# A new table of shifts in the order of a conv-attention block on one core

## The chip, the core and the metric

The kernel runs on one core of one Trainium2 chip. A core has five engines with a queue of instructions each: TensorE (PE in the profile, with its weight loads as PEld), VectorE (DVE), ScalarE (ACT), GpSimd (POOL) and SyncE (SP, which here only issues DMAs). They work at the same time and wait for each other through semaphores; each takes its own instructions strictly in the order in which they were written. The metric is the device time in microseconds of one execution, as the median of several runs.

## The reference

The input `x` is 16 images of 128 channels and 96 x 96 pixels in fp32. Per image:

```python
xn1 = layernorm(x)                       # over the channels of each pixel
q, k, v = xn1 @ wq.T, xn1 @ wk.T, xn1 @ wv.T     # 8 heads of 16 channels
q, k = l2norm(q), l2norm(k)              # over the 9216 pixels
attn = softmax(q @ k.T * 16 ** -0.5)     # 16 x 16 per head
x = x + (attn @ v) @ wp.T
xn2 = layernorm(x)
h1 = w_in @ xn2                          # 128 -> 512 channels
h2 = conv3x3(h1, w_dw)                   # one filter per channel, zero padding
x = x + w_out @ gelu(h2)                 # 512 -> 128 channels
```

The attention is over channels: its matrix is 16 x 16 per head and has to be summed over all pixels of an image before it can be applied to any.

## The kernel before

An image is cut into 8 bands of 12 rows (1152 pixels), a band into 3 units of 4 rows (384 pixels). Three streams of work run interleaved over the whole kernel:

- **First norm and attention of the next image** (`norm(i, False)`, line 789, and `attention`, line 997). A band is loaded by SP (`load_a`), transposed by PE (`forth_a`), copied by ACT (`copied_a`), its statistics taken by DVE (`stats_a`), the inverse deviation made by POOL (`variance_a`, `power_a`) and applied (`scaled_a`); PE adds it to a Gram matrix (`gram`) and transposes it back (`back_a`), and ACT places it in a ring of rows in SBUF (`place_a`).
- **Second norm of the image at hand** (`norm(i, True)`): PE applies the attention as one 128 x 128 matrix (`mix`), ACT moves the result to SBUF (`mixed`), a DMA that POOL issues adds `x` to it (`add_x`), and then come `forth_b`, `stats_b`, `variance_b`, `power_b`, `back_b` and `place_b`, the last on DVE.
- **The feed-forward part**, in *jobs*: one job is one band and one chunk of 128 of the 512 hidden channels (`conv_job`, line 1133). PE makes the hidden rows (`hidden`, line 1152), ACT copies them out of PSUM (`kept`, line 1157, and `halo`, line 1148, for rows shared with the next band). The nine taps of the 3 x 3 filter are shared among engines: two or three, sometimes four, are made by ACT as products (`products`, line 1168) into buffers `pr`; POOL adds the first of them to the middle tap (`merge`, lines 1171 and 1174); DVE makes the others one after the other in PSUM (`tap`, lines 1180 and 1184), the first of them on top of the merged tile, and the last into a buffer `h3`; two DMAs issued by POOL add the rest, one product to another (`add_last`, line 1193) and their sum to `h3` (`add_first`, line 1196). ACT then applies GELU (`gelu`, line 1201). In some bands the fourth chunk is made by nine matmuls on PE instead (`by_matmuls`, line 1249: `conv` and `conv_gelu`, with the bias of the first and last column applied by ACT from a tile `edge`). Finally PE multiplies all four chunks by `w_out` (`out`, line 1300), DVE adds the result to `x` (`add`, line 1307), and SP stores the band (`store`).

There are 467 jobs. Buffers are few: 4 PSUM banks `h` for PE's results, 8 `pr`, 8 `h3`, 4 `zT`, 5 + 2 bands of `x`.

**The order.** The program is not written in the order in which it runs. Every piece is handed to a planner (`Plan`, line 223) with its engine, an estimated duration, what it reads and writes, and a *place*. `Plan.order` (line 269) plays the execution through with those estimates: when an engine is free, it takes from the pieces that are ready the one with the lowest place; buffers are handed out in the order of the places too. The order so found is then emitted, and on the chip each engine follows it as a fixed list, whatever the real durations are.

The place of a piece is made in `place_at`, line 546: the number of the job beside which it belongs, plus a constant for its kind (`AT`), plus a *shift* for its kind in this stretch of 15 jobs (`SHIFTS`), and a `RANK` that counts for the engine but not for the buffers.

```python
def place_at(kind, place, i=1):
    of = kind if i else kind + "_0"
    return Place(place + (AT[of] + SHIFTS.get(max(0, int(place // STRETCH)), {}).get(of, 0)), RANK.get(kind, 0))
```

A stretch spans 15 places, while many of the constants and shifts are hundreds or thousands: so within a stretch the kinds of one engine are in most cases strictly ranked, and a shift takes effect where it moves a kind past another kind of the same engine. For `out` and `hidden` on PE, for example, `AT` has 421.1 and 416.95. For `add_first` and `merge` on POOL it has -1420.85 and -380.8.

Of the kernel before, what the change touches and what calls it, by code (L numbers as in the profile page):

```python
# [51 lines left out]
    load_w=-385.3, weights=-616.15, zeros=-141.7, load_a=-42.4, forth_a=-588.2, stats_a=1671.35, variance_a=269.75,  # L52
# [14 lines left out]
    0: dict(load_w=-0.4, weights=5.2, zeros=-2.2, load_a=1.4, forth_a=-37.4, stats_a=-4.5, variance_a=-15.2,  # L67
        power_a=-1.9, merge=29.7, scaled_a=690.3, gram=-4.7, place_a=179.4, attention=-230.7, mix=-831.2,
        residual=407.9, mixed=-700.9, stats_b=8.5, variance_b=533.1, power_b=17.1, back_b=0.1, place_b=508.2,
        kept=1387.1, products=-11.5, add_last=-9.9, tap=-0.8, add_first=-4.2, gelu=16.5, conv=-3.5, conv_gelu=1.4,  # L70
        out=0.1, add=-1520.8, store=-31, mix_0=46.9, residual_0=637.6, gram_0=-6.5, forth_a_0=1.3, forth_b_0=1.7,
        stats_b_0=1195.7, scaled_a_0=1.5, copied_a=-135, back_a_0=1.7, back_b_0=-17.1, place_a_0=-6.5, late=-10.3,
        load_a_0=1.9, load_dw=15.2, units=-13.6, variance_a_0=49.8, power_a_0=-208.3, variance_b_0=5.2,
        power_b_0=545.9),
    1: dict(load_a=0.9, forth_a=-9.5, stats_a=-0.1, variance_a=121.4, power_a=-0.2, merge=7.6, scaled_a=1062.4,
        gram=1.4, back_a=-389.8, place_a=-1619.2, attention=-0.8, mix=-12.3, mixed=433.4, add_x=767.6, forth_b=9.1,
        stats_b=-189.7, variance_b=-0.3, power_b=5.7, back_b=-0.2, place_b=-2, halo=-3.8, hidden=0.4, kept=2503.9,
        add_last=13.5, tap=0.1, add_first=-18.8, gelu=2.7, conv=6.5, conv_gelu=1.1, add=-969.7, store=315.5),
    2: dict(load_a=0.2, forth_a=1, stats_a=21, variance_a=148.9, power_a=-29.3, merge=3.4, scaled_a=224.7,
        gram=369.1, back_a=0.3, place_a=21.5, mix=0.5, add_x=761.8, stats_b=-602.5, variance_b=-0.6, power_b=221.3,  # L80
        back_b=-2.3, place_b=864.3, halo=60.3, kept=2.2, products=-0.4, tap=0.1, add_first=-63.4, gelu=48.9,
        conv=-1.5, conv_gelu=-0.2, out=-0.2, add=5.4, store=-860.5, copied_a=-16.2, copied_b=451.4),
# [4 lines left out]
    4: dict(load_a=0.4, forth_a=-0.8, stats_a=51.7, variance_a=-21.1, power_a=-8.5, merge=0.5, scaled_a=17.6,  # L87
        gram=2.7, place_a=24.1, mix=0.1, add_x=38.9, forth_b=-7, stats_b=608, variance_b=-3.1, power_b=-2,
        place_b=1309.5, halo=-1008.9, hidden=0.7, kept=-17.1, add_last=15.7, tap=-0.6, add_first=-2.4, gelu=-118.4,
        conv=-5.9, conv_gelu=-0.5, out=0.6, add=14.9, store=-14.5, copied_a=1563.7),  # L90
    5: dict(load_a=-0.3, forth_a=-1.1, stats_a=-4.6, variance_a=-285.1, power_a=20.3, merge=-1017.1,
        scaled_a=-11.2, gram=-3.8, back_a=4.5, place_a=13.1, attention=-1.5, mixed=-1.7, add_x=314.7, stats_b=-3.5,
        variance_b=2352.2, power_b=0.1, place_b=-11.9, halo=-12.3, kept=5.1, products=-0.1, add_last=61.6,
        tap=-1.5, add_first=-47.3, gelu=14.1, conv=0.9, conv_gelu=-1.2, out=-1, add=-1511.4, copied_a=-616.3,
        copied_b=-1294.4),
    6: dict(load_a=0.4, forth_a=-2.4, stats_a=-5.7, variance_a=-1678.1, power_a=-1.9, merge=0.8, scaled_a=1445.1,
        place_a=952, mix=-3, mixed=-0.4, add_x=28.1, forth_b=0.7, stats_b=-0.6, variance_b=819.8, power_b=-4,
        place_b=872.4, kept=2426.6, products=0.1, add_last=38.2, tap=-0.1, add_first=11, gelu=41.2, conv=-0.4,
        conv_gelu=0.2, out=13.2, add=565, store=-118.5, copied_a=-10.5),
    7: dict(load_a=1.9, stats_a=15.2, variance_a=-1.3, power_a=31.3, merge=-6.8, scaled_a=22.7, gram=-2644.1,  # L100
        back_a=-3.3, place_a=-207.8, attention=2.2, mix=-0.9, stats_b=4, variance_b=-5.6, power_b=277.8,
        place_b=1322.6, halo=4.2, kept=1343, products=1.2, add_last=18.7, tap=-0.3, add_first=-69.9, gelu=-2.4,
        conv=0.3, conv_gelu=-0.5, out=-0.6, add=-2068, store=1612, copied_a=412.3, copied_b=483.1),
    8: dict(load_a=7.2, forth_a=0.5, stats_a=-7.7, variance_a=11.4, power_a=-406.1, merge=-42.2, scaled_a=-0.4,
        gram=19.8, back_a=0.2, place_a=-12.5, mix=0.5, mixed=-562.6, add_x=779.6, forth_b=15.6, power_b=16.9,
        back_b=-1235.4, halo=-16.2, hidden=-0.6, kept=477.2, products=-0.2, add_last=8.3, tap=0.3, add_first=13.3,
        conv=3342, conv_gelu=0.1, add=-2.7, store=-3.9, copied_a=-3.4),
    9: dict(forth_a=0.4, stats_a=20.3, variance_a=4367.7, power_a=42.6, merge=-0.1, scaled_a=1020.8, gram=-4.3,
        back_a=-1129, place_a=1, mix=1.8, mixed=4.9, add_x=-38.6, forth_b=-0.3, variance_b=-9.2, power_b=64,
        back_b=0.1, place_b=-452.4, halo=6.1, kept=518.8, add_last=797.1, tap=0.1, add_first=58.8, gelu=0.8,  # L110
        conv=-3.1, add=-1766.3, store=7, copied_a=1422.9),
    10: dict(load_a=6.8, forth_a=0.9, variance_a=-29.3, power_a=1.7, merge=-7.6, scaled_a=1431.4, gram=10.5,
        place_a=0.2, mixed=113.1, add_x=581.8, forth_b=-1.8, stats_b=-0.6, variance_b=1573.4, power_b=1638.8,
        place_b=8.5, halo=13.6, hidden=-0.1, kept=12.3, add_last=482.1, tap=0.1, add_first=0.3, gelu=-0.1,
        conv_gelu=1.2, out=-0.2, add=7.3, store=-988, copied_b=53.2),
    11: dict(load_a=-2.7, forth_a=-4.3, stats_a=1830.9, variance_a=-291.5, power_a=37.2, merge=-23.5,
        scaled_a=-0.9, gram=-4.9, back_a=1.5, place_a=184.8, attention=-2.9, add_x=-2.7, stats_b=-201.5,
        variance_b=1.5, back_b=-0.3, place_b=1.9, halo=-4528.6, hidden=-1.1, kept=-260, products=-0.7,
        add_last=25.2, tap=0.5, add_first=-0.7, gelu=34.8, conv=-22.2, conv_gelu=0.7, add=-957.7, store=-1469.1,
        copied_a=-742.1),  # L120
# [1264 lines left out]
```

## Time and profile before

| | |
|---|---|
| median of three runs | 3978.27 us (3977.37 to 3985.19) |
| the profiled execution | 3984.49 us |
| its span, first to last instruction | 3982.8 us |
| mean granted clock of TensorE | 0.998 |
| instructions | 50,559 |
| moved by DMA | 777.37 MB, mean 195 GB/s |

The span is the time from the first to the last instruction of one profiled execution; the time of a run has a little around it. A row of a group names the line of the kernel, the engine, the operation, the tile written and the tiles read, the count, the busy time and the mean of one in ns, and then how long the engine stood idle just before such instructions and for whom. A row of the view by stretches gives the window, its length, and the busy time and instruction count of each engine, then the granted clock, the busy share of the 16 DMA engines and their GB/s. A row of the waits says which engine waited at which line for what, the total in us, how often, and the longest.

### The profile page before, as it was taken

What the parts mean: (1) busy time and instruction counts of PE and PEld (TensorE: products, weight loads), DVE (VectorE), ACT (ScalarE), POOL (GpSimd) and SP (SyncE); (2) the same over time, 40 slices, a digit from 0 to 9 for tenths busy, and PEclk for the clock granted to TensorE, in tenths of its full rate; (3) what the DMA queues carried; (4) which work ended last, traced back from release to release, by engine and by line L of the source; (5) the groups of instructions that cost most, each with busy time, mean ns of one, the idle gap of its engine ahead of it and who ended that gap; (6) DMA issues with size and microseconds to landing.
All of it is one profiled execution on the core that took longest, in us unless ns stands there. A gap on an engine that the chain in (4) does not pass through costs nothing.

```text
span 3982.8 us, 50559 instructions
## 1 busy us (share of the span) xinstructions
PE 3851.3 (97%) x16467; PEld 2484.8 (62%) x16467; DVE 3828.5 (96%) x4392; ACT 3604.9 (91%) x5478; POOL 3378.8 (85%) x3107
## 2 busy tenths in 40 slices
PE   8999999999999999999999999999999999999899
PEld 7566666666666666666666665666666666665555
DVE  7999999999999999999999999999999999999888
ACT  3999989989999999999999999998999999999887
POOL 5998889889898988988888898888988989888674
PEclk9999999999999999999999999999999999999999
DMA  3999999999999999999999999999999998999887
GB/s 99 185 202 211 190 204 194 207 191 196 212 191 213 205 193 206 199 214 196 190 204 201 209 195 193 208 197 202 199 194 202 201 211 183 217 197 182 178 168 165
DMA packets 191688, 777.37 MB, mean 195 GB/s; under 512 B 22208, under 2 KB 23616, under 8 KB 191424
## 3 DMA queue, kind: packets, MB, share of 16 engines
q0 software_dynamic: 151920, 622.33, 82.2%
q1 hardware_dynamic: 38784, 151.75, 10.3%
q8 instruction: 129, 2.11, 0.2%
q14 instruction: 135, 1.11, 0.1%
q10 hardware_dynamic: 720, 0.07, 0.0%
HBM read 148.85 MB, written 75.50 MB: 56 GB/s over the span
## 4 chain that ended last, share of the span: by engine, by line
PE 38%; DVE 14%; ACT 13%; DMA 8%; POOL 8%; issue 6%; POOLq 0%; DVEq 0%; ACTq 0%
PE h L1300 11%; PE h L1152 9%; PE h L1264 9%; DVE acc L1184 7%; ACT pr L1168 6%; DMA h<-pr 6%; DVE acc L1180 3%; PE h L808 3%; DVE h L1180 2%; PE h L954 2%; POOL merged L1171 2%; PE g L906 2%; ACT h L1157 2%; DMA pr<-pr 2%; PE h L858 2%
## 5 line engine op out<-in xcount | busy, mean ns | idle before, releaser
L1168 ACT ACTIVATE pr<-h,ratio 128x1152 f32<-128x1152 f32 x1494 | 1841.0, 1276 | 31.8 <-DMA h<-pr 9.9
L1184 DVE SCALAR_TENSOR_TENSOR acc<-h,ratio,acc 128x1152 f32<-128x1152 f32 (+1 forms) x1308 | 1810.3, 1384 | 7.7
L1171 POOL TENSOR_TENSOR merged<-pr,h 128x1152 f32<-128x1152 f32 x466 | 1236.7, 2654 | 112.4 <-DVE acc L1180 51.4
L1152 PE MATMUL h<-xn,winT 128*128 128x384 f32 (+2 forms) x2802 | 1083.0, 494 | 22.2 <-ACT h L1157 12.7
L1300 PE MATMUL h<-h,woutT 128*128 128x384 f32 x3072 | 1074.8, 488 | 9.0 <-ACT h L1157 4.9
L1264 PE MATMUL h<-xn,comp 128*128 128x380 f32 (+2 forms) x2430 | 895.1, 483 | 7.2 <-DVE st_b L866 2.6
L1300 PEld LDWEIGHTS h<-h,woutT 128*128 128x128 f32 x3072 | 569.0, 190 | 385.8 <-ACT h L1157 13.8
L1157 ACT COPY h<-h 128x384 f32<-128x384 f32 (+2 forms) x1401 | 654.2, 498 | 145.0 <-PE h L1152 141.9
L1180 DVE SCALAR_TENSOR_TENSOR acc<-h,ratio,merged 128x1152 f32<-128x1152 f32 x466 | 684.0, 1468 | 32.7 <-POOL merged L1174 16.6
L1152 PEld LDWEIGHTS h<-xn,winT 128*128 128x128 f32 x2802 | 497.7, 190 | 342.5 <-issue 35.8
L1201 ACT ACTIVATE h<-h,ksum 128x1152 f32<-128x1152 f32 (+1 forms) x586 | 617.7, 1086 | 70.8 <-DMA h<-pr 68.7
L1196 POOL DMA_DIRECT2D h<-pr x466 | 465.1, 999 | 252.5 <-DVE h L1180 56.8
L1180 DVE SCALAR_TENSOR_TENSOR h<-h,ratio,acc 128x1152 f32<-128x1152 f32 x467 | 655.1, 1403 | 3.4 <-PE h L1300 0.2
L1264 PEld LDWEIGHTS h<-xn,comp 128*128 128x128 f32 x2430 | 432.0, 189 | 242.7 <-issue 14.2
L1193 POOL DMA_DIRECT2D pr<-pr x466 | 484.5, 1057 | 86.3 <-ACT pr L1168 66.7
L875 POOL TENSOR_TENSOR ve_b<-ve_b,mhalf 128x4 f32<-128x4 f32 x288 | 369.0, 1282 | 8.6
L899 POOL TENSOR_TENSOR zT<-zT,ve_a 128x512 f32<-128x512 f32 x270 | 342.0, 1275 | 7.0
L875 POOL TENSOR_TENSOR ve_a<-ve_a,mhalf 128x4 f32<-128x4 f32 x288 | 333.3, 1165 | 13.5
L858 PE MATMUL h<-ident,x 128*128 128x128 f32 x2244 | 318.6, 276 | 26.9 <-ACT h L1157 8.2
L858 PEld LDWEIGHTS h<-ident,x 128*128 128x128 f32 x2244 | 261.7, 142 | 113.9 <-issue 33.7
L906 PEld LDWEIGHTS g<-zT 128*128 128x128 f32 x2160 | 272.9, 192 | 46.1 <-POOL zT L899 13.3
L808 PE MATMUL h<-xn,mwT 128*128 128x384 f32 x768 | 291.1, 491 | 10.1 <-ACT x L817 2.2
(187 smaller groups left out, 3947.3 us busy)
## 6 DMA issues: line engine op xcount, KB each, us to landing
pr<-pr POOLq DMA_DIRECT2D x466, 576.0 KB, 7.8
h<-pr POOLq DMA_DIRECT2D x466, 576.0 KB, 7.9
x<-in_x_dram SPq DMA_DIRECT2D x128, 576.0 KB, 7.3
out_dram<-x SPq DMA_DIRECT2D x127, 576.0 KB, 4.8
x<-in_x_dram POOLq DMA_DIRECT2D x123, 576.0 KB, 8.9
out_dram<-x SPq DMA_DIRECT2D x3, 192.0 KB, 1.9
h<-in_L_conv_w_in_dram SPq DMA_DIRECT2D x1, 256.0 KB, 3.3
h<-in_L_conv_w_out_dram SPq DMA_DIRECT2D x1, 256.0 KB, 3.5
```

The lines of the kernel that those rows point to most:

```text
L858: nc.tensor.transpose(d["pT", q][:, k, :], xt[:, j * P : (j + 1) * P], ident)
L875: nc.gpsimd.tensor_tensor(rstd, rstd, mhalf, ALU.pow)
L1152: nc.tensor.matmul(rows(ph), lhsT=winT[:, n, :], rhs=window(xn, r0 + r, e - r, 1), start=True, stop=True)
L1157: nc.scalar.copy(window(h1_, r, e - r, 1), rows(d.pop(("ph", r))))
L1168: nc.scalar.activation(to, shifted(t), AF.Copy, scale=ratio[:, n, t : t + 1])
L1171: nc.gpsimd.tensor_tensor(merged, d["pr", dma_taps[0]], shifted(UNIT), ALU.add)
L1180: nc.vector.scalar_tensor_tensor(to, shifted(t), ratio[:, n, t : t + 1], also, ALU.mult, ALU.add)
L1184: nc.vector.scalar_tensor_tensor(to, shifted(t)[:, lo:hi, cut], ratio[:, n, t : t + 1], to, ALU.mult, ALU.add)
L1193: nc.gpsimd.dma_start(out=d["pr", dma_taps[1]], in_=d["pr", t], accum_op=ALU.add)
L1201: nc.scalar.activation(h3, h3, AF.Gelu, bias=ksum[:, z, n : n + 1])
L1264: nc.tensor.matmul(d["pc"][:, lo:hi, cut], lhsT=comp[:, t, :], rhs=window(xn, r0 + dy, UR, dx)[:, lo:hi, cut], start=(t == order[0]), stop ...
L1300: nc.tensor.matmul(rows(d["po"]), lhsT=woutT[:, n, :], rhs=h3s[g, n][:, s * UR : (s + 1) * UR, :], start=(k == 0), stop=(k == NCH - 1),)
```

## The change

Only `SHIFTS` (line 66) is replaced, by a table of the same form: 32 stretches, about 30 kinds in each. All other constants, the functions and the computation are the same. Of 1021 entries that either table has, 1005 differ; 242 entries of the old and 361 of the new are larger than 100 either way. Two stretches of the old and the new table in full, the last lines of stretch 0, and the shift of `add_first` where it went up most:

```diff
     0: dict(
...
-        load_a_0=1.9, load_dw=15.2, units=-13.6, variance_a_0=49.8, power_a_0=-208.3, variance_b_0=5.2,
-        power_b_0=545.9),
+        copied_a=-1469.5, back_a_0=-4.7, back_b_0=8.2, place_a_0=184.5, place_b_0=-6.4, late=-53.4, load_dw=3811.7,
+        units=36, variance_a_0=3610.5, power_a_0=-1224.6, variance_b_0=-20.3, power_b_0=1317.8),
...
-    3: dict(load_a=4.1, stats_a=-23.7, variance_a=-225.4, power_a=762, merge=-499.1, scaled_a=275.8, gram=17.8,
-        place_a=-222.9, attention=2.7, mix=-2.4, mixed=507.5, add_x=722, forth_b=6.4, stats_b=-607.4,
-        variance_b=1.6, power_b=208, place_b=4, halo=-5114.5, kept=1.1, products=0.1, add_last=-33.4,
-        add_first=-2.7, gelu=-3397, conv=-9, conv_gelu=-0.6, add=568.1, store=-17.6, copied_a=1164.2),
+    3: dict(load_a=4.1, forth_a=1.7, stats_a=-4, variance_a=149, power_a=1353.6, merge=22.5, scaled_a=-15.5,
+        gram=-37.3, place_a=-606.9, attention=3, mix=-3.3, add_x=364.7, forth_b=2.6, stats_b=-15.6, variance_b=-1,
+        power_b=-35.1, back_b=-419.8, halo=-4560.9, hidden=-409.4, add_last=351.8, add_first=1417.6, gelu=-2921.3,
+        conv=-6.4, conv_gelu=0.3, add=-12.8, store=-0.3, copied_a=-12.1),
...
-    29: dict(mix=-1.5, mixed=-15.9, add_x=-4.2, forth_b=-32.8, stats_b=-24.1, variance_b=1162.7, power_b=2838.3,
-        back_b=17.8, place_b=-6.3, halo=43.2, hidden=224.5, kept=-25.7, products=-1.3, add_last=34.8, tap=-0.2,
-        add_first=0.2, gelu=-4563.5, conv=-9.6, conv_gelu=1.1, out=170.7, add=-3.3, copied_b=-13.3),
+    29: dict(merge=-1.4, mix=13.3, mixed=-1627, add_x=3.2, forth_b=-12.1, stats_b=-1151.7, variance_b=0.8,
+        power_b=-29.4, back_b=50.4, place_b=906.3, halo=-4600.5, hidden=-475.1, kept=1529.1, products=2,
+        add_last=1967.8, tap=1.3, add_first=4901, gelu=-4636.8, conv=2.3, conv_gelu=0.4, out=194.6, add=-1787.8,
+        store=-629.6, copied_b=51),
```

| stretch | `add_first` before | `add_first` after | `merge` before | `merge` after |
|---|---|---|---|---|
| 3 | -2.7 | 1417.6 | -499.1 | 22.5 |
| 7 | -69.9 | 338.8 | -6.8 | -1050.5 |
| 15 | 10.4 | 1826.8 | -369.3 | -4.9 |
| 16 | -3.3 | 1473.5 | 337.1 | 23.5 |
| 18 | -64.3 | 1823 | -15.7 | 3871.9 |
| 20 | 53.2 | 1839 | 13.3 | -4.6 |
| 21 | -3.5 | 5992.8 | 1.4 | -22 |
| 25 | 6.1 | 1363.9 | 0.5 | -46.2 |
| 29 | 0.2 | 4901 | 0 | -1.4 |
| 30 | 0 | 3068.2 | 4905.7 | -0.4 |
| 31 | 0 | 4907.6 | 8.4 | 3850.3 |

In stretch 30, `hidden` goes from 4 to 0.1 and `out` from -1343.5 to -428.

More of the change, by code (lines that the diff above doesn't have):

```diff
@@ L75 @@
[L75 to L82, printed above, removed]
@@ L91 @@
[L91 to L99, printed above, removed]
@@ L100 @@
[L100 to L115, printed above, removed]
@@ new lines @@
+    5: dict(load_a=-1.2, forth_a=-1, variance_a=-629.1, power_a=20.3, merge=-1022.6, scaled_a=1349.9, gram=27.4,
+        back_a=-422.4, place_a=1446.3, attention=-1.7, mix=1, mixed=3.4, add_x=-417.5, forth_b=13.5, stats_b=577.3,
+        variance_b=1620.2, power_b=-18.7, back_b=-0.1, place_b=-0.7, halo=-3293.3, hidden=-0.3, kept=18.2,
+        products=0.6, add_last=0.4, tap=0.6, add_first=-4, gelu=-2.5, conv=-0.3, conv_gelu=-1, out=-0.1,
+        add=-615.5, store=1.5, copied_a=-0.1, copied_b=-1286.4),
@@ new lines @@
+    30: dict(merge=-0.4, mix=192.9, mixed=1563.7, add_x=-44.9, forth_b=33.8, stats_b=4.1, variance_b=2765.5,
+        power_b=1412, back_b=3.4, place_b=1313.9, halo=-4519.1, hidden=0.1, kept=6.2, products=2, add_last=33.1,
+        tap=0.3, add_first=3068.2, gelu=-48.6, conv=-10, conv_gelu=1, out=-428, add=-601.5, store=-4.8),
+    31: dict(merge=3850.3, hidden=-0.2, kept=4295.2, products=1.1, tap=402.3, add_first=4907.6, gelu=-5949.9,
+        conv=-11.3, conv_gelu=3477.9, out=2968.8, add=-5.3, store=-425.9),
```

212 lines of the change are left out of this document (124 added, 88 removed).

## The prediction

> **What bounds the kernel now.** I read the page first, for how full each engine is.
>
> ```profile
> span 3982.8 us, 50559 instructions
> PE 3851.3 (97%) x16467; PEld 2484.8 (62%) x16467; DVE 3828.5 (96%) x4392; ACT 3604.9 (91%) x5478; POOL 3378.8 (85%) x3107
> q0 software_dynamic: 151920, 622.33, 82.2%
> q1 hardware_dynamic: 38784, 151.75, 10.3%
> L1184 DVE SCALAR_TENSOR_TENSOR acc<-h,ratio,acc 128x1152 f32<-128x1152 f32 (+1 forms) x1308 | 1810.3, 1384 | 7.7
> L1171 POOL TENSOR_TENSOR merged<-pr,h 128x1152 f32<-128x1152 f32 x466 | 1236.7, 2654 | 112.4 <-DVE acc L1180 51.4
> L1180 DVE SCALAR_TENSOR_TENSOR acc<-h,ratio,merged 128x1152 f32<-128x1152 f32 x466 | 684.0, 1468 | 32.7 <-POOL merged L1174 16.6
> L1201 ACT ACTIVATE h<-h,ksum 128x1152 f32<-128x1152 f32 (+1 forms) x586 | 617.7, 1086 | 70.8 <-DMA h<-pr 68.7
> ```
>
> PE, DVE, the 16 DMA engines (82.2% + 10.3%) and ACT are all above 90%. No single engine is the bound: what is left to win is only the time in which PE and DVE stand still. So the second view is busy time by stretches, to see where they do.
>
> ```profile
> core 0: us, PE busy (x) PEld busy (x) DVE busy (x) ACT busy (x) POOL busy (x), PEclk, DMA share, GB/s
> 0.00:100.00 100.00, 88.73 (x590) 71.58 (x591) 73.30 (x187) 34.41 (x72) 55.34 (x112) 1.00 0.33 100
> 100.00:200.00 100.00, 90.86 (x402) 58.84 (x401) 96.47 (x109) 95.35 (x143) 92.22 (x83) 1.00 0.91 185
> 500.00:1000.00 500.00, 483.72 (x2090) 315.12 (x2089) 482.85 (x548) 459.90 (x699) 437.46 (x398) 1.00 0.95 199
> 1000.00:1500.00 500.00, 487.72 (x2098) 314.72 (x2097) 491.65 (x558) 468.70 (x714) 442.78 (x401) 1.00 0.96 203
> 1500.00:2000.00 500.00, 488.23 (x2094) 316.03 (x2093) 488.79 (x549) 465.27 (x707) 435.10 (x400) 1.00 0.96 201
> 2000.00:2500.00 500.00, 485.00 (x2085) 313.46 (x2084) 482.31 (x550) 462.60 (x704) 433.86 (x397) 1.00 0.95 200
> 2500.00:3000.00 500.00, 487.35 (x2092) 314.43 (x2091) 486.98 (x552) 464.84 (x705) 440.11 (x400) 1.00 0.96 201
> 3000.00:3500.00 500.00, 487.21 (x2096) 314.64 (x2095) 486.32 (x552) 464.19 (x707) 437.23 (x398) 1.00 0.96 201
> 3700.00:3840.00 140.00, 128.04 (x437) 73.57 (x436) 120.25 (x127) 111.25 (x161) 91.23 (x78) 0.99 0.92 186
> 3840.00:3952.00 112.00, 110.80 (x369) 65.30 (x368) 109.77 (x100) 98.31 (x142) 80.98 (x59) 1.00 0.90 182
> ```
>
> Each 500 us window of the middle has PE idle for 11.8 to 16.3 us and DVE for 8.3 to 17.7. Two windows are worse than the others (500 to 1000 and 2000 to 2500), and one place is much worse: 3700 to 3840, where PE stands still for 12.0 us and DVE for 19.8. The granted clock is 0.99 to 1.00 in all of them, so it plays no part.
>
> The third view, waits, says for whom DVE and ACT waited.
>
> ```profile
> DVE x L1307 <- PE h L1300: 33.2, 36, 3.8
> DVE xn L958 <- PE h L954: 17.9, 25, 2.5
> DVE acc L1180 <- POOL merged L1174: 16.6, 15, 6.6
> DVE acc L1180 <- POOL merged L1171: 9.7, 10, 1.5
> ACT h L1157 <- PE h L1152: 141.9, 186, 5.0
> ACT h L1201 <- DMA h<-pr: 68.7, 58, 3.2
> POOL h L1196 <- DVE h L1180: 56.8, 47, 3.2
> ```
>
> DVE waits for results of PE (33.2 and 17.9 us) and for POOL's merge (16.6 + 9.7 = 26.3 us). POOL in turn stands in front of the DMA issue of line 1196 (`add_first`) until DVE has made the last tap, and whatever POOL has behind that issue, a merge above all, waits with it.
>
> **The change part by part.** No operation is added or removed: the same 50,559 instructions, bytes and buffers. A shift only moves a kind of operation up or down the queue of its own engine within one stretch of 15 jobs. Adding up `AT`, `RANK` and the shift for each kind and stretch in both tables, and sorting, I find: PE's kinds change places in 63 of 1152 pairs, DVE's in 31 of 320 with the taps first in all 32 stretches of both tables, ACT's in 250 of 1440, POOL's in 318 of 1152, SP's loads and stores in 12 of 32. So it is mainly POOL and ACT that get another order, and what it is worth is what it does to the idle time of PE and DVE.
>
> *Step 1, stretch 29.* Before, `out` (421.1 + 170.7 = 591.8) stands ahead of `hidden` (416.95 + 224.5 = 641.5) on PE in stretches 29 and 30; after, `hidden` is ahead in 29 (-58 against 616) and still behind in 30. Jobs 435 to 449 are the 140 us window above, and the timeline shows the price:
>
> ```profile
> 3763.24 7.12 PE L1300 MATMUL h<-h,woutT 128*128 128x384 f32 x16 [0.38 <-DVE xn L958]
> 3770.19 2.38 PE L1152 MATMUL h<-xn,winT 128*128 128x384 f32 x6
> 3771.04 0.48 ACT L1157 COPY h<-h 128x384 f32<-128x384 f32 x1 [5.00 <-PE h L1152]
> 3772.80 0.85 POOL L1196 DMA_DIRECT2D h<-pr  x1 [8.85 <-PE h L1152]
> 3773.37 2.75 POOL L1171 TENSOR_TENSOR merged<-pr,h 128x1152 f32<-128x1152 f32 x1
> 3778.86 1.43 DVE L1180 SCALAR_TENSOR_TENSOR acc<-h,ratio,merged 128x1152 f32<-128x1152 f32 x1 [6.59 <-POOL merged L1174]
> ```
>
> Sixteen output matmuls run for 7.12 us, the hidden ones behind them, ACT idles 5.00 us for the first of these, and DVE 6.59 us for the merges that follow. PE's idle time here is 140 - 128.04 = 12.0 us; at the rate of the window 3000 to 3500 (12.79 in 500) it would be 3.6, so 8.4 too much. The next window has 1.2 in 112 where that rate gives 2.9: 1.7 was made up. Net 6.7; bounds 0 (the dip comes from something else, and stays) and 12 (all of PE's idle time there). I take 6, because `out` must then wait instead and its `add` on DVE with it.
>
> *Step 2, the two worse windows.* PE's idle time in the four good 500 us windows is 12.28, 11.77, 12.65 and 12.79, mean 12.4; in the two bad ones 16.28 and 15.00. Nearly every entry of the table differs there too (1005 of 1021 in all), and a new order has no reason to hit the same holes: 3.9 + 2.6 = 6.5 gained. DVE's numbers would say 11.7 (17.15 and 17.69 against a mean of 11.6); I take PE's, as the nearer to the end of the chain. Lower bound 0, or below it if the new order is bad there.
>
> *Step 3, `add_first` behind `merge` on POOL.* Before, line 1196 goes ahead of the merge in every stretch. After, it has been pushed behind it in stretches 3, 7, 15, 16, 20, 21, 25, 29 and 30 (shifts of +339 to +5993), some 135 jobs. There a merge no longer stands behind an issue that waits for DVE. At most DVE's 26.3 us of waits for merges go; nine stretches of 31 make it 7.6, and part is counted in step 1 already: I take 3, bounds 0 and 7.6. What is late next is the sum `h3` itself: the DMA starts later by a merge (2654 ns) and GELU (line 1201) and `out` behind it. I cost that at nothing; its cover is that GELU is placed last but for a few kinds on ACT, that there are 8 `h3` buffers, and that only 58 of 586 GELUs waited for this DMA. If the cover is gone it is the second rival.
>
> *Step 4, what the new order spoils.* The best window (DVE idle 8.3 us in 1000 to 1500) has no reason to stay the best either: back to the mean of 11.6 it gives 3.2 back. Bounds 0 and 10, if all four good windows fall to the middle of good and bad.
>
> *Step 5, parts at nothing.* The start (0 to 200) has new shifts too, among them `load_dw` by +3811.7, so that SP issues it behind every load that is ready. Seven loads of image 0 have buffers and go first in both tables, so its place stays. The cover is the work of the start; if it were late, it would be by its own
>
> ```profile
> dw<-in_L_conv_w_dw_dram SPq DMA_DIRECT2D x1, 18.0 KB, 9.0
> x<-in_x_dram SPq DMA_DIRECT2D x128, 576.0 KB, 7.3
> ```
>
> landing, +9.0 us; on the other side PE's idle time in 100 to 200 can go, -9.1. Loads behind stores on SP would cost 7.3 us for a load that comes too late; they are issued ahead by whole bands (five and two buffers), so nothing. ACT's inversions (`place_a`, `mixed`, `kept`) change nothing that I can point to beyond steps 2 and 4.
>
> *Sum.* -6 - 6.5 - 3 + 3.2 = -12.3 us. The profiled execution took 3984.49 us (1.7 around its span) and lies 6.2 above the median of the runs, 3978.27. 3984.49 - 12.3 = 3972.2, and less the 6.2: **3966 us**, 0.9969 of before.
>
> **The rivals.**
>
> *A wash (about 3978).* A new order closes some holes and opens as many. DVE's idle times over the six windows of 500 us (17.15, 8.35, 11.21, 17.69, 13.02, 13.68) have a standard deviation of 3.6 us; two independent draws over seven such windows differ by 3.6 x square root of 14 = 13 us either way. For it: most small shifts in either table move nothing, and steps 2 and 4 are the same argument with two signs. Against it: steps 1 and 3 have places in the trace.
>
> *Late sums (slower, 3990).* In the 135 jobs of step 3 each `h3` DMA starts at least a merge later, and with the DMA engines 0.95 busy it also lands later. Today those jobs' share of the GELU waits is 135/467 x 68.7 = 20 us. Were that doubled, and half of DVE's waits for the output matmuls in these jobs (33.2 x 135/467 = 9.6) added once more, since `out` and its `add` stand behind GELU, it would be 20 + 4.8 = +24: -12.3 + 24 = +12, 3990. It decides once more than 12.3 us come through, about 0.09 us for each of the 135 jobs. For it: the chain of waits already has DMA `h<-pr` in it.
>
> ```profile
> by line: PE h L1300 10.8%; PE h L1152 9.0%; PE h L1264 8.8%; DVE acc L1184 6.7%; ACT pr L1168 6.0%; issue 5.9%; DMA h<-pr 5.8%; DVE acc L1180 2.6%; PE h L808 2.5%; DVE h L1180 2.4%; PE h L954 2.4%; POOL merged L1171 2.3%; PE g L906 2.2%; AC
> ```
>
> Against it: 528 of 586 GELUs find their data there.
>
> *More collisions of merge and first tap (slower, 3990).* The first tap has two inputs in SBUF and so has the merge:
>
> ```profile
> L1171 POOL TENSOR_TENSOR merged<-pr,h x466: 2413/2535/4153, 85.2 to 3949.9; 128x1152 f32<-128x1152 f32 x156
> L1180 DVE SCALAR_TENSOR_TENSOR acc<-h,ratio,merged x466: 1396/1417/3149, 87.7 to 3952.6; 128x1152 f32<-128x1152 f32 x156
> ```
>
> Minimum, median and longest stand in ns: a first tap can take 3149 where 1417 is usual, a merge 4153 where 2535 is. Over 466 first taps the mean is 1468 on the page, so 466 x 51 = 24 us are lost to it today. POOL's order changes most of all, and were the loss doubled, -12.3 + 24 = +12. Against it: the order of POOL against DVE was not kept free of it before either; a redraw should leave 24 as it is. The Trainium skill, "SBUF — State Buffer", section "SBUF: two separate sides", says why order alone sets this: a DVE operation with two SBUF inputs and a GpSimd operation that reads SBUF exclude each other for the whole instruction, and whichever starts second is blocked. By that rule, a longest first tap of 1417 + up to 2535 is possible, and the trace agrees with its 3149. [...]
>
> *A larger gain (3947).* Step 1 at 12, step 2 at 11.7, step 3 at 7.6, step 4 at nothing: -31.3, and 3984.5 - 31.3 - 6.2 = 3947.
>
> **How the numbers follow.** About 0.2%, 8 us, is what a measurement of this kernel can tell from no change: faster is under 3970, slower over 3986. The forecast (3955 to 3975) has 0.38; the larger gain 0.10; the wash 0.28, of which 0.08 falls below 3970 and 0.08 above 3986; late sums 0.15, collisions 0.05; 0.04 is left for edits that cancel. Faster: 0.36 + 0.10 + 0.08 = 0.54. Slower: 0.08 + 0.15 + 0.05 = 0.28. The rest, 0.18, within. The range goes from 3944 (a little below the larger gain) to 3996 (late sums with a quarter more), which leaves out about 2 in 10; the forecast's own is 3955 to 3975.
>
> **What the profile after would show.** Step 1: PE idle in the last 280 us under 16 us, no DVE wait for a merge near 6.59 us, hidden matmuls ahead of output ones in jobs 435 to 449. Step 2: no 500 us window with PE idle above 14 us. Step 3: POOL's wait `h L1196 <- DVE h L1180` falls by a third from 56.8, DVE's waits for merges under 24 us; wrong if ACT's wait for DMA `h<-pr` grows beyond 80 us. Collisions: the mean first tap stays within 20 ns of 1468. Busy times of PE and DVE should stay within 1%. The forecast is wrong if PE and DVE idle as much as now, in other places.

## The result, and the profile after

The new table makes the kernel faster by 0.29%: 3968.99 us median (3965.78 to 3975.59, nine runs) against 3979.84 (3975.59 to 3985.19, nine runs) of the kernel before, run beside it, a ratio of 0.9971 with a 95% interval of 0.9961 to 0.9982. The forecast was 3966, or 0.9969. The gain came from the end of the kernel, where the forecast had put half of it.

The page of the kernel after. The line numbers are higher by 14, since the table is longer; line 1194 here is 1180 before, 1185 is 1171, 1215 is 1201.

```profile
span 3968.9 us, 50596 instructions
PE 3849.0 (97%) x16467; PEld 2482.4 (63%) x16467; DVE 3832.0 (97%) x4392; ACT 3605.0 (91%) x5478; POOL 3390.7 (85%) x3107
L1185 POOL TENSOR_TENSOR merged<-pr,h 128x1152 f32<-128x1152 f32 x466 | 1239.9, 2661 | 102.2 <-DVE acc L1194 48.5
L1194 DVE SCALAR_TENSOR_TENSOR acc<-h,ratio,merged 128x1152 f32<-128x1152 f32 x466 | 683.9, 1468 | 33.8 <-POOL merged L1188 13.9
L1215 ACT ACTIVATE h<-h,ksum 128x1152 f32<-128x1152 f32 (+1 forms) x586 | 616.9, 1085 | 53.7 <-DMA h<-pr 49.5
```

The engines do the same work: PE is busy for 2.3 us less and DVE for 3.5 us more, and a first tap takes 1468 ns as before. The page has 50,596 instructions where the prediction had the same 50,559; the 37 more are all semaphore operations: of matmuls, vector, scalar and GpSimd work and DMAs there are as many as before. What fell is idle time. The same stretches of time as in the prediction, of the kernel after (PE is the first of the busy times, DVE the third):

```profile
core 0: us, PE busy (x) PEld busy (x) DVE busy (x) ACT busy (x) POOL busy (x), PEclk, DMA share, GB/s
500.00:1000.00 500.00, 487.31 (x2067) 312.77 (x2067) 485.07 (x547) 461.58 (x700) 435.83 (x393) 1.00 0.95 200
1000.00:1500.00 500.00, 480.24 (x2048) 309.44 (x2048) 479.15 (x542) 460.57 (x699) 431.31 (x392) 0.99 0.94 196
1500.00:2000.00 500.00, 490.05 (x2115) 317.69 (x2114) 494.50 (x557) 465.81 (x712) 443.66 (x404) 1.00 0.96 202
2000.00:2500.00 500.00, 488.86 (x2106) 314.05 (x2106) 488.09 (x559) 468.13 (x711) 443.98 (x403) 1.00 0.97 204
2500.00:3000.00 500.00, 489.68 (x2116) 316.34 (x2115) 488.47 (x554) 468.17 (x708) 442.18 (x402) 1.00 0.96 203
3000.00:3500.00 500.00, 486.49 (x2085) 313.65 (x2084) 489.69 (x555) 468.75 (x713) 440.15 (x402) 1.00 0.96 202
3700.00:3840.00 140.00, 134.08 (x463) 78.92 (x462) 137.59 (x140) 127.17 (x184) 104.53 (x85) 1.00 0.98 196
3840.00:3952.00 112.00, 111.89 (x377) 66.96 (x376) 105.86 (x100) 85.41 (x129) 67.18 (x51) 1.00 0.83 170
3952.00:3983.00 31.00, 13.35 (x43) 7.78 (x42) 4.78 (x6) 3.26 (x10) 0.00 (x0) 0.98 0.10 38
```

The two bad windows (500 to 1000 and 2000 to 2500) became good: PE idles 12.7 and 11.1 us there where it idled 16.3 and 15.0. But the window 1000 to 1500, the best one for DVE before, became the worst: PE idles 19.8 us and DVE 20.9. A window of fixed times tells how busy the engines were, not how far the program had come; for that a marker is needed. From 3700 on PE is now busy for 259.32 us of 268.9, so it idles 9.6 us. The last window of the kernel before, which the prediction did not need, completes its sum:

```profile
3952.00:3983.00 31.00, 27.00 (x86) 15.89 (x84) 21.31 (x20) 10.05 (x24) 2.94 (x4) 0.98 0.40 96
```

128.04 + 110.80 + 27.00 = 265.84 of 282.8: before, PE idled 17.0 us from 3700 on. Of the 13.9 us between the two spans, 7.4 are thus idle time of PE after 3700; the other 6.5 are work of PE that was already done by then (259.32 us left against 265.84).

The best marker of progress is the first tap of a job, of which there are 467. These two rows of DVE's timelines are the 436th of each kernel (job 435, where stretch 29 begins), counted in the trace, before and then after:

```profile
3700.18 1.43 DVE L1180 SCALAR_TENSOR_TENSOR acc<-h,ratio,merged 128x1152 f32<-128x1152 f32 x1
```

```profile
3698.61 1.43 DVE L1194 SCALAR_TENSOR_TENSOR acc<-h,ratio,merged 128x1152 f32<-128x1152 f32 x1
```

Of the 13.9 us between the two spans (3982.8 and 3968.9), 1.6 are won in the 435 jobs up to there, 93% of the kernel, and 12.3 in the last 32 jobs.

The waits of the kernel after that answer to those shown of before (33.2, 17.9, 16.6, 9.7, 141.9, 68.7 and 56.8 there):

```profile
DVE x L1321 <- PE h L1314: 27.1, 31, 3.1
DVE xn L972 <- PE h L968: 10.5, 14, 2.2
DVE acc L1194 <- POOL merged L1188: 13.9, 17, 2.5
DVE acc L1194 <- POOL merged L1185: 11.3, 13, 1.9
ACT h L1171 <- PE h L1166: 137.4, 176, 4.7
ACT h L1215 <- DMA h<-pr: 49.5, 43, 6.1
POOL h L1210 <- DVE h L1194: 54.6, 38, 7.1
```

DVE waits less for PE (13.5 us), and as long for merges as before (25.2 against 26.3); its longest wait for one is 2.5 us where it was 6.6. That total hides two changes with opposite signs. Up to 3690 us, ahead of the end, these waits became longer; the rows from 88 to 3690 us, before and then after:

```profile
DVE acc L1180 <- POOL merged L1171: 8.6, 9, 1.5
DVE acc L1180 <- POOL merged L1174: 8.5, 13, 1.5
```

```profile
DVE acc L1194 <- POOL merged L1188: 13.0, 16, 2.5
DVE acc L1194 <- POOL merged L1185: 11.3, 13, 1.9
```

They went from 17.1 to 24.3 us there (22.2 in a second trace of the new kernel, E12), and from 9.2 to 0.9 us in what is left.

### The profile page after: what moved, and what is told of

It reads as the page before. It is cut to its first block, busy times and chain, and to the rows that moved or that the text cites. A ratio compares the mean times of both kernels' runs of the same rounds, so it can differ in the third digit from the quotient of the medians.

```text
span 3968.9 us, 50596 instructions
## 1 busy us (share of the span) xinstructions
PE 3849.0 (97%) x16467; PEld 2482.4 (63%) x16467; DVE 3832.0 (97%) x4392; ACT 3605.0 (91%) x5478; POOL 3390.7 (85%) x3107
## 4 chain that ended last, share of the span: by engine, by line
PE 24%; DVE 10%; ACT 5%; POOL 4%; DMA 4%; issue 3%; DVEq 0%; POOLq 0%; ACTq 0%
PE h L1314 7%; PE h L1166 6%; PE h L1278 6%; DVE acc L1198 5%; ACT pr L1182 2%; DMA pr<-pr 2%; DVE acc L1194 2%; DVE h L1194 2%; DMA h<-pr 2%; PE h L822 2%; PE h L968 1%; POOL merged L1185 1%; PE h L872 1%; PE g L920 1%; POOL merged L1188 1%
## 5 line engine op out<-in xcount | busy, mean ns | idle before, releaser
L1194 DVE SCALAR_TENSOR_TENSOR acc<-h,ratio,merged 128x1152 f32<-128x1152 f32 x466 | 683.9, 1468 | 33.8 <-POOL merged L1188 13.9
L1210 POOL DMA_DIRECT2D h<-pr x466 | 476.2, 1022 | 236.6 <-DVE h L1194 54.6
L1215 ACT ACTIVATE h<-h,ksum 128x1152 f32<-128x1152 f32 (+1 forms) x586 | 616.9, 1085 | 53.7 <-DMA h<-pr 49.5
L889 POOL TENSOR_TENSOR ve_b<-ve_b,mhalf 128x4 f32<-128x4 f32 x288 | 377.8, 1325 | 7.9
L889 POOL TENSOR_TENSOR ve_a<-ve_a,mhalf 128x4 f32<-128x4 f32 x288 | 349.2, 1214 | 10.9
```

Source lines behind the costliest of these rows:

```text
L889: nc.gpsimd.tensor_tensor(rstd, rstd, mhalf, ALU.pow)
L1194: nc.vector.scalar_tensor_tensor(to, shifted(t), ratio[:, n, t : t + 1], also, ALU.mult, ALU.add)
L1215: nc.scalar.activation(h3, h3, AF.Gelu, bias=ksum[:, z, n : n + 1])
```

## The experiments

Two theories stood at the start. *Tail*: the tables are worth the same over the first 435 jobs, and the gain is in the entries of stretches 29 to 31. *Redraw* or *path*: a table works only as a whole, and a part of it is worth nothing elsewhere. Four kernels cut the table in pieces.

**E1.** The old table with the last three stretches of the new one:

```diff
-    29: dict(mix=-1.5, mixed=-15.9, add_x=-4.2, forth_b=-32.8, stats_b=-24.1, variance_b=1162.7, power_b=2838.3,
...
+    29: dict(merge=-1.4, mix=13.3, mixed=-1627, add_x=3.2, forth_b=-12.1, stats_b=-1151.7, variance_b=0.8,
...
```

> The kernel before with the entries of stretches 29, 30 and 31 alone taken from the new table. Tail theory (the two tables are worth the same up to job 435, and the whole gain sits in the last three stretches, because PE no longer runs dry there): 10 to 16 us faster than before, about 3967, with PE idle under 8 us in the window 3700 to 3840. Redraw theory (a table's gain belongs to the path as a whole; entries made for another history are worth nothing by themselves): within 5 us of before. By the planner's own estimate this order ends 9.5 us earlier than before's.

Measured: 3975.24 us, ratio 0.9986 (0.9977 to 0.9995), 5.6 us faster. That is about half of the gain, and neither theory's number. PE idles 8.5 us in the window 3700 to 3840 (131.53 busy), where the tail theory had under 8.

**E2.** The old table without its last three stretches:

```diff
-    29: dict(mix=-1.5, mixed=-15.9, add_x=-4.2, forth_b=-32.8, stats_b=-24.1, variance_b=1162.7, power_b=2838.3,
...
-    30: dict(merge=4905.7, mix=52.8, mixed=-886.1, add_x=-1116.3, forth_b=-395, stats_b=2889.8, variance_b=5686.3,
...
-    31: dict(merge=8.4, hidden=-420.1, kept=5422.3, products=1098.8, gelu=-4942.6, conv=0.1, conv_gelu=4561.5,
-        out=4165, add=-980.4, store=1117.3),
```

> The kernel before with no shifts at all in stretches 29 to 31 (places there from AT alone). If the new tail entries are good, this is as slow as before or slower: 3980 to 3990. If instead the old tail entries were bad (output matmuls ahead of hidden ones in 29 and 30, merges last on POOL in 30), dropping them gives the whole gain: 3965 to 3970. The planner's own estimate is 10.0 us less than before's.

Measured: 3968.39 us, ratio 0.9969 (0.9958 to 0.998). The whole gain is there without a single new number. So the old entries of the end were worse than none.

**E3.** The new table without its last three stretches:

```diff
-    29: dict(merge=-1.4, mix=13.3, mixed=-1627, add_x=3.2, forth_b=-12.1, stats_b=-1151.7, variance_b=0.8,
...
-    30: dict(merge=-0.4, mix=192.9, mixed=1563.7, add_x=-44.9, forth_b=33.8, stats_b=4.1, variance_b=2765.5,
...
-    31: dict(merge=3850.3, hidden=-0.2, kept=4295.2, products=1.1, tap=402.3, add_first=4907.6, gelu=-5949.9,
...
```

> The new kernel with no shifts in stretches 29 to 31. Tail theory in its strict form (the new tail entries make the gain): it is lost, 3978 to 3984. If only the old tail entries were bad, it stays: 3966 to 3972. The planner's own estimate is 0.8 us more than before's and 8.2 more than the new kernel's.

Measured: 3976.23 us, ratio 0.9987 (0.9978 to 0.9997), between the two numbers. The new middle without an end of its own is no better than the old one: it is slower than E2, which differs only in the first 29 stretches.

**E4.** No shifts at all:

```diff
 SHIFTS = {
-    0: dict(load_w=-0.4, weights=5.2, zeros=-2.2, load_a=1.4, forth_a=-37.4, stats_a=-4.5, variance_a=-15.2,
...
-        out=4165, add=-980.4, store=1117.3),
 }
```

> No shifts in any stretch. Theory that shifts are worth on the chip what they are worth in the planner's play: its estimate is 66.7 us more than before's, so about 4046. Theory that the order on the chip is a redraw each time, whatever the planner thinks: within 13 us of before, 3967 to 3993. By stretches of 15 jobs the first has every stretch longer by some 2 us, the second only scatter.

Measured: 4043.01 us, ratio 1.0157 (1.0143 to 1.0171), 62.5 us slower, where the planner's estimate had 66.7. The table is worth 1.6%, and the planner's play says so to within 5 us. But not every stretch is longer, as that theory had it: of the 29 up to job 435, 17 are longer than before and 12 are not.

The next four asked what within the tables does it.

**E5.** Step 1 alone, one number:

```diff
-        back_b=17.8, place_b=-6.3, halo=43.2, hidden=224.5, kept=-25.7, products=-1.3, add_last=34.8, tap=-0.2,
+        back_b=17.8, place_b=-6.3, halo=43.2, hidden=-475.1, kept=-25.7, products=-1.3, add_last=34.8, tap=-0.2,
```

> The kernel before with one number changed: `hidden` in stretch 29 from 224.5 to -475.1, so that PE takes the hidden matmuls ahead of the output matmuls there. Step 1 as the prediction put it (this order is what makes the dip at 3764): 6 us faster than before, bounds 0 and 12, and PE's idle time in the window 3700 to 3840 falls from 12 to about 4. Rival (the dip comes from the whole set of entries of that stretch): within 3 us of before, with the dip still there or moved. The planner's own estimate is 1.3 us less.

Measured: 3977.21 us, ratio 0.9984 (0.9976 to 0.9993), 6.4 us faster. The time is the one expected, but the trace does not bear out the reason. The stretches of time at the end of this kernel:

```profile
3700.00:3840.00 140.00, 130.52 (x452) 74.86 (x451) 132.12 (x135) 119.86 (x173) 97.38 (x81) 1.00 0.95 191
3840.00:3952.00 112.00, 110.85 (x367) 65.64 (x366) 99.61 (x93) 88.41 (x130) 68.89 (x54) 1.00 0.83 171
3952.00:3983.00 31.00, 20.71 (x66) 11.89 (x64) 15.99 (x16) 7.15 (x17) 0.86 (x1) 0.97 0.24 65
```

DVE is busier by 11.9 us in the first window (132.12 against 120.25), and the dip at 3764 is gone: DVE's waits for that merge in this window, before and then in E5, are

```profile
DVE acc L1180 <- POOL merged L1174: 8.1, 2, 6.6
```

```profile
DVE acc L1180 <- POOL merged L1174: 0.7, 1, 0.7
```

Yet PE's idle time there went from 12.0 to 9.5, not to 4, and over the whole end from 17.0 to 15.9 (262.09 busy of 278.0). Jobs 435 to 449 take 122.3 us in place of 139.8, and the next sixteen 136.9 in place of 120.0. From the first tap of job 450 to the end, before and then in E5:

```profile
3840.03:3983.00 142.97, 137.77 (x453) 81.16 (x451) 131.08 (x119) 108.33 (x164) 83.92 (x62) 1.00 0.79 164
3818.78:3978.00 159.22, 150.78 (x503) 89.19 (x501) 134.85 (x128) 115.25 (x175) 85.93 (x67) 1.00 0.75 155
```

What the taps gain, PE pays back: it has 13.0 us more of work left at that point (150.78 against 137.77), mostly the filters that it makes itself (200 matmuls against 178) and the norms (70 against 45), with 144 output matmuls in both. By the trace this number is worth 1.1 us at the end (282.6 to 281.5 us from job 435 on). The remaining part of the 6.4 lies in front of it, where PE takes the same matmuls in the same order (the first 15,496 of 16,467), and stays open. One trace cannot place a difference of this size there: the way from the first tap to that of job 405, on which the order is the same before and in E1, E2, E5, E9 and E10, took between 3357.7 and 3371.2 us in their six traces.

**E9.** The old table without stretch 29 alone:

```diff
-    29: dict(mix=-1.5, mixed=-15.9, add_x=-4.2, forth_b=-32.8, stats_b=-24.1, variance_b=1162.7, power_b=2838.3,
-        back_b=17.8, place_b=-6.3, halo=43.2, hidden=224.5, kept=-25.7, products=-1.3, add_last=34.8, tap=-0.2,
-        add_first=0.2, gelu=-4563.5, conv=-9.6, conv_gelu=1.1, out=170.7, add=-3.3, copied_b=-13.3),
```

> The kernel before with the entries of stretch 29 taken out, those of 30 and 31 left. If the entries of stretch 29 alone made the end of the kernel slow, this gives the same as taking out all three stretches: 9 to 14 us faster than before. If those of 30 (output matmuls first, merges last on POOL) had a share, it gives less than two thirds of that: under 8 us. The planner's own estimate is 9.7 us less.

Measured: 3968.73 us, ratio 0.9962 (0.9949 to 0.9974), 15.1 us faster. All that taking out the three stretches gave at the end (E2: 272.0 us from job 435 on) came from this one entry of 22 numbers, taken out as a whole (271.6 us; before 282.6):

```profile
3700.00:3840.00 140.00, 137.42 (x474) 80.07 (x474) 137.90 (x143) 125.61 (x182) 103.25 (x86) 1.00 0.96 195
3840.00:3952.00 112.00, 111.45 (x373) 66.77 (x372) 100.85 (x93) 85.77 (x130) 63.78 (x48) 1.00 0.78 161
3952.00:3983.00 31.00, 8.09 (x25) 4.21 (x23) 4.68 (x6) 1.81 (x4) 0.00 (x0) 0.96 0.10 38
```

PE idles 2.6 us in the first window and 8.4 over the end. Stretch 30, where `out` is still ahead of `hidden` and the merges are last on POOL, costs nothing measurable. The end accounts for 11.0 of the 15.1 us; the rest is not there and stays open, as in E5.

**E8.** Step 3 at the end of the kernel, in the new table:

```diff
     29: dict(
...
-        add_first=4901,
+        add_first=0.2,
     30: dict(
...
-        add_first=3068.2,
+        add_first=0,
     31: dict(
...
-        add_first=4907.6,
+        add_first=0,
```

> The new kernel with `add_first` of stretches 29, 30 and 31 set back to the old values 0.2, 0 and 0, so that the DMA that completes h3 is issued ahead of the merges again, at the end alone, where no later stretch can suffer. Step 3 as predicted (issues behind merges spare DVE waits): 1 to 3 us slower than the new kernel, about 3971. Late sums (the rival: sums that come earlier spare waits): 1 to 5 us faster than the new kernel, 3964 to 3968. The planner's own estimate is 1.8 us more than the new kernel's.

Measured: 3971.44 us, ratio 0.9969 (0.9956 to 0.9983), which is the new kernel's 0.9971. Neither step 3 nor the rival of late sums shows: from job 435 on it takes 271.3 us, the new kernel 270.3 and 270.0 in its two traces.

**E6.** Step 3 in the middle, one number in the old table:

```diff
     3: dict(
...
-        add_first=-2.7, gelu=-3397, conv=-9, conv_gelu=-0.6, add=568.1, store=-17.6, copied_a=1164.2),
+        add_first=1417.6, gelu=-3397, conv=-9, conv_gelu=-0.6, add=568.1, store=-17.6, copied_a=1164.2),
```

> The kernel before with one number changed: `add_first` in stretch 3 from -2.7 to 1417.6, the new table's value, so that it stands behind `merge` on POOL for 15 jobs. Local theory (step 3 of the prediction: a shift is worth what it does to the waits of its own stretch): within 2 us of before. Path theory (the shifts of the later stretches fit one exact run of the play, and are worth less than nothing once it has been left): every stretch after the third longer, and by the planner's estimate 184 us more than before, about 4165, slower even than with no shifts at all (4043).

Measured: 4166.61 us, ratio 1.0458 (1.0443 to 1.0472). One number of 887 costs 182 us; the local theory is out. The page and the waits of this kernel:

```profile
span 4171.1 us, 50544 instructions
PE 3927.5 (94%) x16467; PEld 2499.8 (60%) x16467; DVE 3858.2 (92%) x4392; ACT 3617.0 (87%) x5478; POOL 3384.1 (81%) x3107
```

```profile
ACT h L1157 <- PE h L1152: 232.1, 243, 6.2
ACT h L1201 <- DMA h<-pr: 97.9, 60, 7.0
POOL h L1196 <- DVE h L1180: 86.1, 57, 4.9
POOL merged L1171 <- ACT pr L1168: 76.3, 40, 6.5
DVE x L1307 <- PE h L1300: 63.9, 66, 3.8
```

It is not one wait that has grown: these five have, by 43 to 92% (141.9, 68.7, 56.8, 46.5 and 33.2 before). The engines do the same work and stand still between, along the whole kernel: stretches 4 to 28 take 121 to 160 us, where the old table has 121 to 129. Not every one is longer, as was expected: 19 of the 25 are. PE's order is that of the kernel before for the first 2300 of its 16,467 matmuls, and another from there on.

**E11.** The same number, with all shifts behind it taken out:

```diff
-        add_first=-2.7, gelu=-3397, conv=-9, conv_gelu=-0.6, add=568.1, store=-17.6, copied_a=1164.2),
+        add_first=1417.6, gelu=-3397, conv=-9, conv_gelu=-0.6, add=568.1, store=-17.6, copied_a=1164.2),
-    4: dict(load_a=0.4, forth_a=-0.8, stats_a=51.7, variance_a=-21.1, power_a=-8.5, merge=0.5, scaled_a=17.6,
...
-        out=4165, add=-980.4, store=1117.3),
```

> As the run with one number changed (`add_first` in stretch 3 at 1417.6), but with all shifts after stretch 3 taken out. Path theory (it was the later shifts, made for another path, that cost 184 us): about as slow as with no shifts at all, 4040 to 4055, so some 115 us faster than with them. If that one number did the harm by itself (a late DMA that goes on hurting): as slow as with them, 4150 to 4180. The planner's estimate is 69 us more than before's.

Measured: 4071.17 us, ratio 1.023 (1.0215 to 1.0245). Taking out 28 stretches of shifts makes the kernel 91 us faster by the two ratios. So most of what E6 lost was lost by the later shifts, as the path theory has it, though the time lies above its 4055.

**E13.** The control, the old table up to stretch 3 and nothing behind:

```diff
-    4: dict(load_a=0.4, forth_a=-0.8, stats_a=51.7, variance_a=-21.1, power_a=-8.5, merge=0.5, scaled_a=17.6,
...
-        out=4165, add=-980.4, store=1117.3),
```

> The control for the run before: the old table as far as stretch 3, `add_first` there at its old -2.7, no shifts after. The planner's estimate is 59.6 us more than before's (9.6 less than with 1417.6). If moving `add_first` in stretch 3 costs next to nothing by itself: 4060 to 4075, as with it. If it does harm that the play does not see: clearly faster than the 4071 with it, 4035 to 4050.

Measured: 4045.86 us, ratio 1.0161 (1.0138 to 1.0183), 25 us less than E11, and within the 4035 to 4050 expected if the number does harm by itself. But the traces do not place it (that of E11 is also of its slowest run, 4082.82 us where the other three took 4068 to 4071): stretch 3 takes 126.3 us with it and 123.9 without, and the rest is spread, stretch 10 at 138.3 against 125.9, but stretch 5 at 126.0 against 138.2. Without later shifts the lengths of stretches 4 to 28 scatter by some 5 us (standard deviation 5.2 and 5.0), so that two such orders, if their stretches were independent, would differ by 5 x square root of (2 x 25) = 35 us by chance, as an estimate. Whether the number costs anything by itself stays open.

**E12.** The new kernel again, for a second trace:

> The new kernel once more, on the same chip as the searched end, for a comparison of the two, and for a second trace: if the length of a stretch belongs to the order and not to chance, stretches 3, 7, 9 and 11 are again the long ones (128 us or more), and 17, 23 and 28 the short ones (about 120). Time: 0.997 of before.

Measured: 3972.5 us, ratio 0.997 (0.9959 to 0.9981). Stretches 3, 7, 9 and 11 take 130.1, 132.2, 133.2 and 128.2 us (129.9, 132.9, 129.9, 128.7 in the first trace), and 17, 23 and 28 take 120.2, 119.1 and 120.2.

**E10.** Another end, found with the planner's play in stretches 28 to 31, over the old table:

```diff
...
-    29: dict(mix=-1.5, mixed=-15.9, add_x=-4.2, forth_b=-32.8, stats_b=-24.1, variance_b=1162.7, power_b=2838.3,
...
+    29: dict(gelu=0, power_a=-1903.3, kept=-28.1, variance_a=0, halo=-743.1, copied_b=0, mixed=0, place_a=-808.7,
+        conv=788.0, store=-2647.0, load_a=-1917.3, gram=-43.4, place_b=1988.9, variance_b=1028.4, merge=670.6,
...
```

> The kernel before with another set of shifts in stretches 28 to 31, searched with the planner's own play, every duration as it stands in the kernel, on top of the old table without its last three stretches. The planner's estimate is 15.6 us less than before's and 8.2 less than the new kernel's. If the planner's estimate is good to a few us on the chip: 13 to 18 us faster than before and 3 to 8 faster than the new kernel. If what is left of the end lies below what the play can tell: as the new kernel, or as the old table without its last three stretches, 10 to 13 us faster than before.

Measured: 3961.33 us (3958.24 to 3963.85), ratio 0.9948 (0.9936 to 0.9961), 20.7 us faster than before. On the same chip the new kernel took 3972.5 (3963.93 to 3974.0); no run of the one reaches into those of the other, if only by 0.1 us. It beats both expectations. The end of it:

```profile
3700.00:3840.00 140.00, 138.47 (x482) 81.65 (x481) 135.26 (x142) 120.83 (x177) 101.94 (x86) 1.00 0.94 189
3840.00:3952.00 112.00, 111.73 (x369) 66.38 (x368) 102.97 (x93) 86.01 (x131) 60.10 (x46) 1.00 0.79 166
3952.00:3983.00 31.00, 0.97 (x3) 0.22 (x2) 0.56 (x1) 0.00 (x0) 0.00 (x0) 0.95 0.03 11
```

PE idles 5.3 us of the 256.5 from 3700 on. Not all of the 20.7 us is the new end: in the traces, 9.9 of the 26.3 us between E10 and the kernel before are already there at job 405, where the order is still the same. From there on E10 takes 511.1 us, before 527.5, E9 514.9 and the new kernel 514.1: the end is worth 16.4 us, close to the planner's 15.6, and 3 to 4 more than the other good ends.

**All of them side by side.** The first three columns of times are counted in the traces by first taps. The estimate is the end that the kernel's planner computes, less that of the kernel before; the measured difference is the ratio less one, times 3980.

| kernel | to job 435, us | 435 to 449 | 450 to the end | estimate | measured |
|---|---|---|---|---|---|
| before | 3612.5 | 139.8 | 142.8 | 0 | 0 |
| after | 3611.1 | 116.7 | 153.6 | -7.4 | -11.5 |
| after again (E12) | 3613.7 | 117.7 | 152.3 | -7.4 | -11.9 |
| E1 old, new end | 3614.7 | 119.8 | 157.3 | -9.5 | -5.6 |
| E2 old, no end | 3605.1 | 117.0 | 155.1 | -10.0 | -12.3 |
| E3 new, no end | 3610.2 | 116.5 | 157.3 | +0.8 | -5.2 |
| E5 `hidden` in 29 | 3608.9 | 122.3 | 159.2 | -1.3 | -6.4 |
| E9 without 29 | 3606.4 | 117.0 | 154.6 | -9.7 | -15.1 |
| E8 new, `add_first` at the end | 3617.8 | 117.7 | 153.6 | -5.6 | -12.3 |
| E10 searched end | 3600.8 | 116.9 | 151.3 | -15.6 | -20.7 |
| E4 no shifts | 3680.2 | 117.3 | 156.7 | +66.7 | +62.5 |
| E13 old to 3 | 3680.8 | 117.0 | 157.6 | +59.6 | +64.1 |
| E11 `add_first` in 3, to 3 | 3720.6 | 116.5 | 156.6 | +69.2 | +91.5 |
| E6 `add_first` in 3 | 3792.6 | 129.7 | 161.5 | +184.2 | +182.3 |

The old middle (before, E1, E2, E5, E9) takes 3605.1 to 3614.7 us to job 435, mean 3609.5; the new one (after twice, E3, E8) 3610.2 to 3617.8, mean 3613.2. The new middle is not faster. From job 435 on, the old end takes 282.6 us, every other end on a whole middle between 268.1 and 277.1, but for E5 with 281.5.

## Why the prediction was right, and where it was not

The time, the sign and the size were right. That the sum comes out so close is luck: step 1 gave 6.3 us more than was taken for it, and the -6.3 of steps 2, 3 and 4 did not come.

*Step 1, stretch 29, -6.* The place was right and the size was off: the term measured -12.3 (282.6 to 270.3 us from job 435 on), the upper bound that the step gave. In PE's idle time, in which the step was worked out, it is -7.4 (17.0 to 9.6 us from 3700 on), near the 6.7; the step did not count that PE could have less left to do by then. The reason was wrong in part. The order of `out` and `hidden` does make the dip that was quoted, and E5 removes it, but what follows then takes longer by nearly as much, and the step had put 6 on that order. It is the entry as a whole that was bad: E9 takes it out, and its end is as short as with all three stretches taken out. What in it besides `hidden` costs the rest was not taken apart further.

*Step 2, the two worse windows, -6.5, and step 4, what the new order spoils, +3.2.* These terms failed: together they came to nothing, where -3.3 was forecast. In the first trace PE's idle time in the two windows fell by 3.6 + 3.9 = 7.5, and over the four good ones it rose by 4.1, of which 1000 to 1500 alone lost 7.5 (12.3 to 19.8 us) where the sign of step 2 was no window above 14. So far that is the forecast. But the second trace of the same kernel (E12) has

```profile
500.00:1000.00 500.00, 484.57 (x2065) 312.16 (x2063) 486.53 (x548) 461.29 (x701) 433.66 (x393) 1.00 0.96 200
1000.00:1500.00 500.00, 479.70 (x2049) 310.04 (x2049) 476.98 (x540) 459.91 (x696) 430.99 (x392) 0.99 0.94 196
2000.00:2500.00 500.00, 487.50 (x2097) 312.90 (x2096) 486.24 (x556) 466.04 (x709) 443.09 (x402) 1.00 0.96 203
```

that is 3.4 us less in the two worse windows and 6.8 more in the four others: all six are 3.4 us better in one trace and 3.5 worse in the other. The step that failed is to take two windows of one trace for holes that a new order closes and to count only one window for what it opens. This was the wash, the first rival, and for 93% of the kernel it is what happened: 1.6 us between the first two traces, and over the five traces of the old middle and the four of the new a mean that is 3.7 us longer, well within their scatter of 10. Its reason, that one order has holes where the other has none, is borne out. The lengths of the stretches before 29 correlate with 0.87 to 0.97 between two executions of the same middle, and with 0.05 to 0.34 between the old and the new one.

*Step 3, `add_first` behind `merge`, -3.* Nothing, and ahead of the end it went the wrong way. POOL's wait at that issue for DVE went from 56.8 to 54.6 us where a third less was expected, DVE's waits for merges from 26.3 to 25.2 where under 24 was; up to 3690 us, where seven of the nine stretches lie, they rose from 17.1 to 24.3. (By the table, `add_first` stands behind `merge` in stretch 31 as well, which has two jobs.) At the end E8 finds no difference. In the middle the question could not be put as the step put it, since moving the one kind changes everything behind it (E6).

*Step 5, the start and the parts at nothing.* Right: the first tap starts at 87.7 us before and at 87.5 after.

*The rivals.* Late sums did not come: ACT's wait for the DMA sums fell from 68.7 to 49.5 us. Collisions did not either: the mean first tap is 1468 ns in both, its longest 3149 and 2758. The rule of the Trainium skill ("SBUF — State Buffer", section "SBUF: two separate sides") that a DVE operation with two SBUF inputs and a GpSimd operation that reads SBUF exclude each other still fits the longest first tap (2758 ns, under the 1417 + 2504 of a median first tap behind a median merge); what is lost, 24 us by the working of the prediction, is the same in both orders. DVE's numbers, which step 2 set aside, would have made it 11.7; DVE's idle time in the two windows fell by 2.2 + 5.8 = 8.0 us in the first trace and by 7.6 in the second.

*What the prediction lacked* is the thing that E6 shows. It costed the shifts one by one, each by the waits of its own stretch. A shift has no price of its own: it decides one turn of the planner's play, every later turn is made in a state that depends on it, and the later shifts of the old table are worth having only in the state that its own earlier ones make: with one number changed ahead of them they cost 91 us (E6 against E11), with none changed they save 64 (E13). The planner's play alone, with no chip in it, says the same (184.2 and 69.2, 59.6). The forecast was spared this because it priced most of the table as a redraw, and because its largest real term lies at the end of the kernel, where little is left to depend on a turn.

## What to carry to other kernels

An order made by a planner with tuned priorities should be judged from the end backwards: what a change does to the last stretches is kept, while over the long middle the new order here closed as many holes as it opened. Such a table is not a set of independent rules. The one number changed in the middle, and the two tables spliced (E1), did worse than leaving the later shifts out, so test a table whole, or cut it only at its end; and try the end without any entries, which here gave as much as the new table. The planner's play with fixed estimates came within 7 us of every difference measured here but one (E11, 22 us), which was good enough to find the end of E10 before anything was run. It is not good enough to rank ends that lie a few us apart: it put E1 level with E2 (-9.5 and -10.0), and they measured -5.6 and -12.3.

## What the runs showed that was not expected

One number moved the time by 4.6%. Two executions of one order go the same way to a few us: stretches 3, 7, 9 and 11 of the new table are the long ones each time. What looks like scatter along a kernel can be its order.

The granted clock went down where the engines wait more. This view gives span and mean granted clock, of the kernel before, then of E4 and of E6:

```profile
die 0 (median of its cores): 3982.8 us, clock 0.998
```

```profile
die 0 (median of its cores): 4039.4 us, clock 0.994
```

```profile
die 0 (median of its cores): 4171.1 us, clock 0.986
```

PE's busy time grew with it, from 3851.3 to 3927.5 us in E6, for the same 16,467 matmuls; that is 2.0%, and the clock is lower by 1.2%. What lowers the clock was not tried.
